# Two-layer graph network on one core: the scratch buffers of e, of adj's tiles and of the turned tiles start at multiples of 256 bytes

## The chip, the cores and the metric

The kernel runs on one core of a Trainium2 chip. The metric is the device time of one execution in microseconds (us). The core has a matrix engine (TensorE, in the profile PE, its weight loads PEld), VectorE (DVE), ScalarE (ACT), GpSimd (POOL) and the SyncE queue (SP), from which nearly all transfers are issued; 16 DMA engines carry them. On-chip memory (SBUF) has 128 partitions; a buffer takes the same byte range in each.

## The reference

The input is x (3327 nodes, 256 features) and a sparse weighted adjacency matrix adj (3327 x 3327). Layer 0 repeats two steps, each with two products: one with a fixed row-normalised matrix R made of adj, and one with an attention matrix A that is computed from the features and cut to each row's largest entries which together make 90% of its sum. Layer 1 is a masked attention of four heads over adj's neighbours.

```python
R = S + jnp.eye(N); R = R / R.sum(-1, keepdims=True)     # S is adj
for n in range(STEPS):                                   # 2 steps
    A = _top_p_attention(Xa, W1, W2, W3)                 # softmax, top-p 0.9 of each row, renormalised
    Xf = R @ Xf
    Xa = A @ Xa
    Z = Z + Xf @ U1[n].T + Xa @ U2[n].T
# layer 1
e = leaky_relu(s[:, :, None] + d[:, None, :], 0.2)       # 4 heads
attn = softmax(where(adj > 0, e, -inf), axis=2)
out = elu(einsum('hij,jhf->ihf', attn, hp))
```

## The kernel before

Rows are worked on in 26 tiles of 128 (3328 with padding). One function, `fast`, holds the whole network. It does not issue instructions as it goes: it hands pieces of work, each with an engine, an estimated length, a rank and its needs, to a planner (`Plan`), and the planner writes out one fixed order for every engine and for the SP queue. Each engine then works through its own list in that order, waiting at semaphores; nothing is reordered at run time. An engine or queue that waits holds up everything behind it in its list.

**A row tile in layer 0** goes like this. TensorE makes the logits (`logits`, L905), ScalarE their exponentials, 128 x 3328 fp32, into a buffer e (`exps`, L920). ScalarE and GpSimd look for the cut-off (`count`, L959; `before`, `step`), VectorE takes the window, sorts and drops what lies below it (`window`, `choose`, `drop`, L1075). The product with the features needs e transposed. For 49 of the 52 row tiles (`BLOCKED`) this is done in two halves: VectorE transposes 32 x 32 blocks in place (`turn_blocks`, L1112), and the blocks are then moved through HBM. For each of three column ranges (g) `put_blocks` (L1116) writes 512 KB from e to the scratch tensor `blocks`, in runs of 1024 bytes per partition and group, and `get_blocks` (L1121) brings it back in four transfers of 128 KB, each into 32 partitions, in runs of 256 bytes:

```python
src = blocks[g, :, :, o * P // 2 : (o + 1) * P // 2].rearrange("g (b s) w -> s (g b) w", b=4)
nc.sync.dma_start(self.e[part, g * PART : (g + 1) * PART].rearrange("p (c w) -> p c w", w=P // 2), src)
```

A row so takes 3 `put_blocks` and 12 `get_blocks`, and TensorE then multiplies straight from e (`attend_blocks`, L1128). There are four buffers e in the pool `epool`; every fifth row uses a fifth buffer of the same size, `qq`, in `wpool`. Besides, `Full` multiplies adj with the features (L1153): `load` (L1147) brings adj's tiles into the pool `apool` (four buffers `at` of 2048 bytes per partition). `etpool` has three buffers `et` of 2048 bytes for tiles that TensorE turned. After a row of step 0 `stage` (L1347) writes its products into one of two buffers `ystage`, whose earlier contents must have been stored by `store` (L1358) first.

**Layer 1** (`attend_neighbours`) reuses the buffers: e, `c` and `rhs` hold exponents, `qq` and `c` broadcast rows, `at` adj's tiles, `et` masks, `junk` and `y` (pool `scr`) small things.

**Where buffers lie.** Pools are laid one behind the other in the order in which they are opened, and each buffer is rounded up to a multiple of 32 bytes. In `wpool` buffers lie in the order in which their names first occur. Byte addresses within a partition in the built program, with the remainder to 256:

| buffer | before | mod 256 | after | mod 256 |
|---|---|---|---|---|
| e, four of 13312 bytes, first at | 151520 | 224 | 151552 | 0 |
| qq, 13312 bytes | 115616 | 160 | 105728 | 0 |
| at, four of 2048 bytes, first at | 214848 | 64 | 204800 | 0 |
| et, three of 2048 bytes, first at | 223040 | 64 | 212992 | 0 |
| junk (3328 bytes) | 204768 | 224 | 219136 | 0 |
| y (6752 bytes) | 208096 | 224 | 222464 | 0 |
| rhs, c, kt | 45824, 72448, 99072 | 0 | unchanged | 0 |
| ystage, two of 2048 bytes, first at | 145504 | 96 | 145536 | 128 |
| kq, three of 512 bytes, first at | 130464 | 160 | 130496 | 192 |
| qg, two of 2048 bytes, first at | 132288 | 192 | 132320 | 224 |
| base (1024 bytes) | 149856 | 96 | 149888 | 128 |

13312 and 2048 are multiples of 256, so that all buffers of a pool share the remainder.

Of the kernel before, what the change touches and what calls it, by code (L numbers as in the profile page):

```python
# [10 lines left out]
F32 = mybir.dt.float32  # L11
# [8 lines left out]
P = 128  # L20
N = 3327
NT = 26
NP = NT * P
# [564 lines left out]
def fast(  # L588
# [58 lines left out]
    with ExitStack() as l0:  # L647
        wpool = l0.enter_context(tc.tile_pool(name="wpool", bufs=1))
        small = l0.enter_context(tc.tile_pool(name="small", bufs=2))
        epool = l0.enter_context(tc.tile_pool(name="epool", bufs=4))  # L650
        scr = l0.enter_context(tc.tile_pool(name="scr", bufs=1))
        apool = l0.enter_context(tc.tile_pool(name="apool", bufs=4))
        etpool = l0.enter_context(tc.tile_pool(name="etpool", bufs=3))
        ps_l = l0.enter_context(tc.tile_pool(name="ps_l", bufs=2, space=PSUM))
        ps_a = l0.enter_context(tc.tile_pool(name="ps_a", bufs=1, space=PSUM))
        ps_x = l0.enter_context(tc.tile_pool(name="ps_x", bufs=2, space=PSUM))
# [5 lines left out]


        kt = wpool.tile([P, 3 * 512 + P], F32, name="kt")
        kks = [wpool.tile([P, P + 2], F32, name=f"kk{k}") for k in range(2)]
        for kk in kks:
            GP.memset(kk[:, :: P + 1], 1.0)
# [6 lines left out]
        for gk in gks:  # L674
            GP.memset(gk, 0.0)
            GP.tensor_copy(gk[:DA, DA + 1 :], ident[:DA, :DA])

        stat = wpool.tile([P, 2, NT], F32, name="stat")
        sig, zadd, cn, cs = (wpool.tile([P, NT], F32, name=n) for n in ("sig", "zadd", "cn", "cs"))
        met = wpool.tile([P, 6, NT], F32, name="met")  # L680
# [1393 lines left out]
def tile_gnn(tc: tile.TileContext, *args):  # L2074
    with tc.tile_pool(name="verdict", bufs=1) as pool:
        again = pool.tile([1, 1], I32, name="again")
        fast(tc, again, *args)
        with tc.If(tc.nc.values_load(again, min_val=0, max_val=1) > 0):
            general(tc, *args)
# [38 lines left out]
```

## Time and profile before

| | us |
|---|---|
| median of 3 runs (lowest to highest) | 2103.17 (2099.91 to 2103.81) |
| the profiled execution | 2100.08 |
| its span, first to last instruction | 2098.2 |
| TensorE busy | 2037.8 |
| VectorE busy | 1729.7 |
| ScalarE busy | 1300.0 |
| GpSimd busy | 990.7 |
| packets of the transfer queue, as a share of 16 engines' span | 66.4% |

The profiled execution is 3.1 us below the median, inside the spread of the runs. Busy time counts overlapping instructions once. A line of the groups reads: source line, engine, operation, what it writes and reads, shape, count, then busy time and mean duration, then the idle time of the engine just before these instructions, and what ended it.

### The profile page before, as it was taken

The numbers are of one execution on the slowest core, as the hardware profiler recorded it, in microseconds if no ns is written. First come the engines' busy times: TensorE is split into PE (matmuls) and PEld (weight loads), VectorE is DVE, ScalarE is ACT, GpSimd is POOL, SyncE is SP. The second block draws the span as 40 slices with busy tenths as digits, with TensorE's granted clock in tenths as the row PEclk, the third lists the DMA queues.
The fourth block names the chain that finished last, engine by engine and source line by source line (L and its number), as shares of the span: only waits on it lengthen the run. The fifth ranks groups of instructions, "written<-read, shape, count | busy, mean of one in ns | idle before, by whom it ended". The sixth has DMA issues, their size and how long they took to land. (4 is left out here: it accounts for less than half of the span.)

```text
span 2098.2 us, 34334 instructions
## 1 busy us (share of the span) xinstructions
PE 2037.8 (97%) x10695; PEld 1415.2 (67%) x10695; DVE 1729.7 (82%) x4105; ACT 1300.0 (62%) x2480; POOL 990.7 (47%) x2170
## 2 busy tenths in 40 slices
PE   8999999999999989989999999999999999999997
PEld 6477777878787778767878787787877333333332
DVE  5689897778876871578998979988987999999895
ACT  5767665666556621777778776778652547465552
POOL 4476654446544630567778777777772000000001
PEclk9999999999999999999999999999999999999999
DMA  4188888678877685697787888887743544453341
GB/s 116 45 190 186 194 180 195 168 152 196 189 183 172 176 186 138 199 232 165 181 189 176 203 188 191 185 191 192 182 126 89 157 141 142 125 147 115 112 127 34
DMA packets 580513, 338.56 MB, mean 161 GB/s; under 512 B 327931, under 2 KB 533281, under 8 KB 580321
## 3 DMA queue, kind: packets, MB, share of 16 engines
q1 hardware_dynamic: 579424, 336.06, 66.4%
q8 instruction: 87, 1.43, 0.3%
q14 instruction: 106, 0.86, 0.1%
q10 hardware_dynamic: 896, 0.21, 0.0%
HBM read 242.86 MB, written 93.05 MB: 160 GB/s over the span
## 5 line engine op out<-in xcount | busy, mean ns | idle before, releaser
L959 ACT ACTIVATE junk<-e,sc 128x3327 fp8e5<-128x3327 f32 x147 | 451.0, 3068 | 31.4 <-POOL sc L996 29.8
L1128 PE MATMUL acca<-rhs,e 128*128 128x256 f32 x1872 | 426.8, 381 | 4.6 <-DMA e<-blocks 4.6
L1128 PEld LDWEIGHTS acca<-rhs,e 128*128 128x128 f32 x1872 | 364.9, 197 | 48.7 <-issue 6.0
L1153 PE MATMUL accf<-c,at 128*128 128x256 f32 x1352 | 316.5, 385 | 17.1 <-DMA at<-in_adjt_dram 8.5
L1153 PE MATMUL accf<-main,at 128*128 128x257 f32 x1352 | 313.3, 381 | 5.4 <-ACT main L1304 2.5
L1153 PEld LDWEIGHTS accf<-c,at 128*128 128x128 f32 x1352 | 252.8, 192 | 67.5 <-DMA at<-in_adjt_dram 10.2
L1153 PEld LDWEIGHTS accf<-main,at 128*128 128x128 f32 x1352 | 250.4, 190 | 54.3 <-issue 11.5
L1022 DVE MAX8 cands<-y 128x8 f32<-128x205 f32 (+1 forms) x832 | 242.9, 361 | 3.6
L1918 POOL TENSOR_TENSOR qq<-qq 128x256 f32<-128x256 f32 x4 | 3.0, 759 | 457.0 <-ACT qq L1914 457.0
L1017 DVE SCALAR_TENSOR_TENSOR y<-e,sc 128x1639 f32<-128x1639 f32 x84 | 165.1, 1965 | 62.9 <-POOL sc L1007 61.7
L920 ACT ACTIVATE e<-pl 128x1024 f32<-128x1024 f32 (+1 forms) x168 | 152.9, 920 | 75.4 <-PE pl L905 74.7
L1752 ACT ACTIVATE et<-at 128x448 bf16<-128x448 f32 (+1 forms) x204 | 112.6, 552 | 128.6 <-DVE e L1763 73.3
L1779 PE MATMUL pl<-e,main 128*64 128x416 f32 x1024 | 190.4, 517 | 0.1
L1075 DVE SCALAR_TENSOR_TENSOR e<-e,thr 128x1024 f32<-128x1024 f32 (+1 forms) x168 | 178.4, 1066 | 2.4 <-DMA at<-in_adjt_dram 0.3
L905 PE MATMUL pl<-kt,qg 64*128 64x512 f32 (+1 forms) x832 | 173.7, 536 | 0.4 <-ACT qq L920 0.4
L1112 DVE STREAM_TRANSPOSE e<-e 128x1024 f32<-128x1024 f32 x117 | 146.1, 1248 | 3.7
L1779 PEld LDWEIGHTS pl<-e,main 128*64 128x64 f32 x1024 | 70.3, 137 | 111.0 <-issue 91.5
L1763 DVE SCALAR_TENSOR_TENSOR e<-c,low,et 128x832 f32<-128x832 f32 x128 | 128.8, 1070 | 6.1 <-issue 3.2
L905 PEld LDWEIGHTS pl<-kt,qg 64*128 64x128 f32 x832 | 71.5, 186 | 83.4 <-issue 76.2
L1751 ACT ACTIVATE at<-at 128x448 f32<-128x448 f32 (+1 forms) x204 | 110.8, 543 | 25.7 <-DMA at<-in_adjt_dram 25.6
L1763 DVE SCALAR_TENSOR_TENSOR e<-qq,low,et 128x832 f32<-128x832 f32 x120 | 120.5, 1073 | 4.1 <-PE accf L1793 2.9
L959 ACT ACTIVATE junk<-qq,sc 128x3327 fp8e5<-128x3327 f32 x35 | 107.4, 3068 | 10.7 <-POOL sc L996 10.4
(550 smaller groups left out, 3540.7 us busy)
## 6 DMA issues: line engine op xcount, KB each, us to landing
at<-in_adjt_dram SPq DMA_DIRECT2D x414, 256.0 KB
blocks<-e SPq DMA_DIRECT2D x117, 512.0 KB
e<-blocks SPq DMA_DIRECT2D x468, 128.0 KB
at<-in_adjt_dram SPq DMA_DIRECT2D x102, 192.0 KB
blocks<-qq SPq DMA_DIRECT2D x30, 512.0 KB
qq<-blocks SPq DMA_DIRECT2D x120, 128.0 KB
at<-in_adjt_dram SPq DMA_DIRECT2D x52, 128.0 KB
ys<-ystage SPq DMA_DIRECT2D x26, 256.0 KB
```

Of the source, the lines that this page charges most:

```text
L905: T.matmul(pl[:, lo : lo + m], qg[self.n, self.i // 4][half, self.i % 4, :], kt[half, 512 * k : 512 * k + m], start=True, stop=True,)
L920: S.activation(to, pl, AF.Exp, accum_out=(self.p0, self.p1, self.p2, self.p3)[k],)
L959: S.activation(junk[:, :N], self.e[:, :N], fn, bias=t, scale=-1.0, accum_out=dst, saturate=False)
L1017: V.scalar_tensor_tensor(self.y[:, : hi - lo], self.e[:, lo:hi], self.up, self.e[:, lo:hi], ALU.is_lt, ALU.mult, accum_out=(self.h0, self. ...
L1022: V.max(self.cands[:, a * PIECES // 2 + k, :], self.y[:, at[k] - lo : at[k + 1] - lo])
L1075: V.scalar_tensor_tensor(piece, piece, self.thr[:, o : o + 1], piece, ALU.is_gt, ALU.mult)
L1112: V.transpose(part, part)
L1128: T.matmul(self.acc, lhs, rhs[self.n][:, j, :], start=(j == 0), stop=stop and j == js[-1])
L1153: T.matmul(self.acc[:, : self.w], self.at[j // JC][:, j % JC, :], self.src[:, j, : self.w], start=(j == 0), stop=(j == NT - 1),)
L1752: S.activation(to, src, AF.Sign)
L1763: V.scalar_tensor_tensor(held["e"][:, k, :], extra["both"][b % 2][:, k, :], low[:, j, k : k + 1], held["mask"], ALU.max, ALU.mult,)
L1779: T.matmul(q["acc"][a][k * FH : (k + 1) * FH, c, :C], main[:, j, h * FH : (h + 1) * FH], held["e"][:, h, c * C : (c + 1) * C], start=(j == 0),
```

## The change

No instruction is changed, and the order of every engine and of the SP queue is the same, instruction by instruction. Only addresses differ. The pool `scr` is opened after `apool` and `etpool` instead of before them; `qq` is named right after `kt`, so that it lies behind it; and a buffer `room` of 32 bytes, which nothing uses, is put into the pool `small`, ahead of its others. The table above shows where the buffers lie before and after. Buffers of `small` move by 32 bytes.

```diff
-        scr = l0.enter_context(tc.tile_pool(name="scr", bufs=1))
         apool = l0.enter_context(tc.tile_pool(name="apool", bufs=4))
         etpool = l0.enter_context(tc.tile_pool(name="etpool", bufs=3))
+        scr = l0.enter_context(tc.tile_pool(name="scr", bufs=1))
...
         kt = wpool.tile([P, 3 * 512 + P], F32, name="kt")
+        wpool.tile([P, NP], F32, name="qq")
...
             GP.memset(gk, 0.0)
             GP.tensor_copy(gk[:DA, DA + 1 :], ident[:DA, :DA])
 
+        small.tile([P, 8], F32, name="room", bufs=1)
         stat = wpool.tile([P, 2, NT], F32, name="stat")
```

## The prediction

> **What bounds the kernel now.** I read the page's totals first, then the stretches, then TensorE's waits.
>
> ```profile
> span 2098.2 us, 34334 instructions
> PE 2037.8 (97%) x10695; PEld 1415.2 (67%) x10695; DVE 1729.7 (82%) x4105; ACT 1300.0 (62%) x2480; POOL 990.7 (47%) x2170
> ...
> L1128 PE MATMUL acca<-rhs,e 128*128 128x256 f32 x1872 | 426.8, 381 | 4.6 <-DMA e<-blocks 4.6
> ...
> L1153 PE MATMUL accf<-c,at 128*128 128x256 f32 x1352 | 316.5, 385 | 17.1 <-DMA at<-in_adjt_dram 8.5
> ```
>
> TensorE is busy for 97%. In the trace's records two of its 128x256 matmuls start 216 ns apart at the median (their 381 ns overlap), wherever their operands lie: e at 224 and qq at 160 beyond a multiple of 256, `at` at 64. So TensorE's own work is fixed, and only its idle time can shrink. The busy times of the stretches say where that is:
>
> ```profile
> 95.00:740.00 645.00, 637.06 (x2946) 501.86 (x2946) 537.25 (x1443) 416.20 (x751) 368.43 (x792) 1.00 0.80 182
> 740.00:760.00 20.00, 12.82 (x54) 11.00 (x53) 13.47 (x37) 5.09 (x5) 10.26 (x23) 0.83 0.69 166
> ...
> 895.00:1560.00 665.00, 644.01 (x3008) 522.72 (x3006) 584.10 (x1604) 496.10 (x846) 506.86 (x1100) 0.99 0.80 184
> ...
> 1575.00:2085.00 510.00, 509.41 (x3621) 207.89 (x3618) 461.83 (x583) 261.83 (x622) 14.96 (x23) 1.00 0.41 120
> ```
>
> The first numbers are the stretch's length and TensorE's busy time, the last two DMA share and GB/s. Layer 1 (1575 to 2085 us) leaves TensorE 0.6 us idle: no transfer can gain anything there. Layer 0 leaves 8 + 7 + 21 us idle in the three others shown, with DMA at 0.69 to 0.80. Who ends that idle time (us in total, times, longest):
>
> ```profile
> PE accf L1153 <- DMA at<-in_adjt_dram: 10.5, 6, 6.2
> PE px L1087 <- ACT ystage L1347: 8.5, 3, 7.2
> ...
> PE acca L1128 <- DMA e<-blocks: 4.6, 6, 1.7
> ...
> PE px L822 <- ACT ystage L1347: 0.7, 1, 0.7
> ...
> PE px L822 <- DMA qg<-kqs: 0.5, 1, 0.5
> ```
>
> 10.5 + 4.6 + 0.5 = 15.6 us end directly with a landing. The 8.5 + 0.7 = 9.2 us behind L1347 are landings too, one step removed. This is the longest:
>
> ```profile
> 743.05 0.38 SPq L1358 DMA_DIRECT2D ys<-ystage  x1
> ...
> 750.99 0.59 ACT L1347 COPY ystage<-px 128x512 f32<-128x512 f32 x1 [9.55 <-DMA ys<-ystage]
> ...
> 751.63 0.69 PE L1087 MATMUL px<-ident,e 128*128 128x128 f32 x2 [7.18 <-ACT ystage L1347]
> ```
>
> The store of `ystage` is issued at 743.05, behind the 12 `get_blocks` transfers (from 733.2) and four adj tiles, and lands nearly 8 us later; ScalarE needs the buffer, and every engine stands still meanwhile. So 15.6 + 9.2 = 24.8 us of TensorE's idle time hang on transfers. That is the most that faster transfers can bring.
>
> **What the Trainium skill says.** "DMA: Bandwidth & Descriptors", section "How a descriptor splits into AXI transactions": an aligned run goes in pieces of 256 bytes, and one that starts off a 256-byte boundary needs a piece more, whose unused part still costs 32-byte beats. The trace agrees weakly on reads: `put_blocks`, 1024 bytes a packet, has a usual median of 48 ns from e (224), 47 ns from qq (160), and packets of x into the aligned `rhs` 46 ns. Section "Where 436 GB/s comes from": a port takes 32 bytes a cycle at 850 MHz, so 256 bytes are 8 cycles, 9.4 ns. "SBUF — State Buffer", section "Door 1: The DMA port swizzle (why `[64,N]` ≈ `[32,N]`)": 32 neighbouring partitions reach 8 of 16 ports. A `get_blocks` transfer writes just 32. The same page, section "SBUF: two separate sides": engines and transfers don't contend. In line with it 216 ns stays 216 ns however DMA is loaded.
>
> **The change part by part.**
>
> *`get_blocks`, the main part.* 588 transfers, 588 x 512 = 301,056 packets of 256 bytes, more than half of all. From 224 each writes 32 bytes up to a boundary and 224 beyond, from 160 it is 96 and 160: two pieces. The packet records show a train of 12 begin with packets of 18 ns, then within about 1 us slow to a median near 31 ns with a steady 680 packets per us while nothing else runs. Over 8 ports that is 85 per us and port, 11.8 ns or 10.0 cycles: 8 for the data and, as I read it, one for each of two pieces. That reading is my inference; no aligned train is in the trace. Aligned there is one piece: 9 cycles if it still costs its one, 8 if nothing: 755 to 850 packets per us. Of a train's 6144 packets some 5000 run at the slow rate: 7.4 us now, 6.6 or 5.9 then: 0.8 to 1.5 us off each of 49 trains. A train can't go below its issue: the shortest 12 issues take 6.2 us, the mean 9.0. Bounds: 0, if the slow rate is HBM's; 1.5 us, above which the data themselves stand. I take 1.1 us.
>
> *`put_blocks`.* 147 x 512 packets, 48 to 46 ns at best: 147 x 512 x 2 / 16 = 9.4 us of 16 engines' time, 64 ns a transfer. I count 0.2 us a row and put it into the same 1.1.
>
> *`at`.* 2048 bytes from 64 take 84 ns, 86 to 88 in a backlog; aligned probably 84 to 85. 0 to 0.05 us a transfer; hidden but in the backlogs already counted. Layer 1's 512-byte packets (27 ns) lie under a TensorE with 0.6 us idle: nothing. If that cover were gone, ScalarE's wait for `at` at L1751, 25.6 us in all, would be next.
>
> *`et`, junk, y, and the engines' accesses.* `et` takes two small loads; otherwise engines use these. DVE's L1763 writes e (224) in 1070 ns and the aligned `rhs` in 1069; ACT's count reads e and qq in 3068 each. I cost these at nothing, with bounds of plus and minus 2 ns a matmul (below). The buffers of `small` stay unaligned: nothing. No wait, issue or order changes, so nothing new is queued behind anything.
>
> *What reaches TensorE.* Each stall can lose at most what its own backlog loses, or itself:
>
> - 295.5 us (1.13, adj tile behind 11 `get_blocks`): 0.9. 546.7 us (0.8, likewise): 0.8.
> - 751.6 us (7.18, above): 1.4, the train and four adj tiles.
> - 907.2 us (6.18, adj tile issued at 902.6, behind eight `get_blocks`): 0.9.
> - 1164.5 and 1243.5 us (1.72 and 1.75): 0.7 and 0.6, four to six transfers being ahead.
> - Five of 0.3 to 1.0 us behind `get_blocks` from 1301 to 1504 us and one at 739 us, 3.8 in all: 1.5, as several wait for the first landings of a train.
> - Two of 0.4 and 0.9 us behind L1347, one of 0.7 at L822, one of 0.5 behind `qg`: 0.9.
>
> Sum 7.7 us. Some of it is not kept: when TensorE is earlier, it may wait at the next point for ScalarE (`main` L1164, 5.4 us) or VectorE (3.1 us). I take off a fifth: 6 us. Against the profiled execution's own 2100.1 us (span 2098.2) that is 2094; this execution lies 3.1 us under the median of the runs, and 2103.2 - 6 = 2097 is the forecast.
>
> **The rivals.**
>
> *The straddling costs nothing that counts (same).* The slow packets could be HBM's doing: every 256 bytes are read there as well, and the same bytes were written a few us before. For it: packets that straddle into `wqk` at the start take 18 ns (but they go to 128 partitions, with no queue at a port). Against it: 10.0 cycles per port is a round number, and a train starts fast and slows, as when room in front of a full port is used up. Or the trains do get shorter, but SP's issue (9.0 us on average for 12) then sets their end. Gain 0 to 3 us: 2101 to 2103.
>
> *More than the trains' ends (faster, larger).* SP's issues slow down inside trains (504 ns median for a `get_blocks`, up to 2262): with less backlog SP runs ahead, and adj tiles behind trains start earlier as well as landing earlier. Then 12 to 16 us of the 24.8 go: 2088 to 2091.
>
> *Slower: the common phase.* Until now e, qq, `at` and `et` started at different places within 256 bytes; afterwards all start at 0, as `rhs` and `c` do. If TensorE's two reads, a weight from e or `at` and a moving row from `rhs` or `c`, met in the same part of SBUF, each of 5408 such matmuls (1872 + 480 + 352 + 1352 + 1352) would take longer. It decides from 0.8 ns each (4.3 us); 2 ns would give 10.8 us, less 6: about 2108. Against: 216 ns at the median for e at 224, qq at 160, `et` and `at` at 64, with three pairings of phases.
>
> **How the numbers follow.** Within about 0.2% (4.2 us) a measurement of this kernel can't be told from no change. The main case, 2092 to 2099, gets 0.50, the larger gain 0.12, the hidden one 0.27, the common phase 0.11. The ends of the first and third meet at 2099: a gain of 4 us. So faster 0.62, same 0.27, slower 0.11. Two in ten may be left out, so the range goes from 2089, within the larger gain, to 2105, the hidden case with the runs' own spread of 2 us; the likeliest case alone has 2092 to 2099.
>
> **What would show it.** A saturated train would run at 755 packets per us or more instead of 680, the 256-byte packets' mean fall from 27.4 ns to 20 to 24, and the queue's share from 66.4% to 60 to 64. `put_blocks` from e would show 46 ns. TensorE's wait at 751 us would end 1 to 2 us earlier after its start, those for `at` and e<-blocks sum to 7 to 11 us instead of 15.1, TensorE's busy time stay at 2038, and layer 1 keep its 510 us. The prediction fails if the rate stays at 680 (HBM then sets it), if trains shorten but TensorE's idle time reappears behind ScalarE or VectorE, or if the matmuls' spacing leaves 216 ns.

## The result and the profile after

The changed kernel takes 2083.95 us (median of 6 runs, 2080.69 to 2085.48) against 2100.62 us for the kernel before, run again beside it (6 runs, 2098.58 to 2103.81): a ratio of 0.9916, 95% interval [0.9904, 0.9929]. That is 16.7 us less, where 6 us less was forecast. The forecast time was 2097, with a range of 2089 to 2105: the direction was right, the size was not, and the time lies below the range. The 6 us had been taken off 2103.2, the median of three runs; taken off 2100.6 they lead to 2094.6, so that 2.5 us of the distance to 2097 come from the base.

The page of the kernel after, its totals and the two groups of matmuls shown before (source lines are two higher now):

```profile
span 2083.6 us, 34334 instructions
PE 2036.4 (98%) x10695; PEld 1417.9 (68%) x10695; DVE 1730.6 (83%) x4105; ACT 1298.7 (62%) x2480; POOL 999.0 (48%) x2170
...
q1 hardware_dynamic: 579424, 336.06, 57.3%
...
L1130 PE MATMUL acca<-rhs,e 128*128 128x256 f32 x1872 | 426.9, 381 | 0.6 <-DMA e<-blocks 0.3
...
L1155 PE MATMUL accf<-c,at 128*128 128x256 f32 x1352 | 315.0, 384 | 13.7 <-ACT main L1166 5.4
```

TensorE's work is what it was: 2036 us busy instead of 2038, 381 ns a matmul. The span is 14.6 us shorter, and 13.2 of these left TensorE's idle time (span less busy time: 60.4 us before, 47.2 after). The transfers carry the same bytes in 57.3% of the engines' time instead of 66.4%. TensorE's waits after the change (us in total, times, longest):

```profile
PE accf L1155 <- ACT main L1166: 5.4, 5, 3.4
PE px L1089 <- ACT ystage L1349: 5.0, 1, 5.0
PE accf L1155 <- DMA at<-in_adjt_dram: 5.0, 1, 5.0
...
PE px L824 <- DMA qg<-kqs: 2.7, 2, 1.7
...
PE acca L1130 <- DMA e<-blocks: 0.3, 1, 0.3
```

The wait behind adj's tiles fell from 10.5 us in six pieces to 5.0 in one, the one for e's blocks from 4.6 us to 0.3, the one behind `ystage` from 9.2 to 5.0. The longest stall, in order of time on SP and around it:

```profile
725.39 6.68 SPq L1123 DMA_DIRECT2D e<-blocks  x12
732.17 1.86 SPq L1149 DMA_DIRECT2D at<-in_adjt_dram  x4
734.12 0.38 SPq L1360 DMA_DIRECT2D ys<-ystage  x1
...
740.64 0.59 ACT L1349 COPY ystage<-px 128x512 f32<-128x512 f32 x1 [7.68 <-DMA ys<-ystage]
741.28 0.69 PE L1089 MATMUL px<-ident,e 128*128 128x128 f32 x2 [4.97 <-ACT ystage L1349]
```

From the first `get_blocks` to the store of `ystage` SP needs 8.7 us (734.12 - 725.39) where it needed 9.9 (743.05 - 733.19), and from that store's issue to ScalarE's start it takes 6.5 us instead of 7.9. The train helps twice: SP gets past it sooner, and what is queued behind it lands sooner.

The packet records of both traces, one row for each size that matters. A train is the 6144 packets of one row's `get_blocks`, from its first packet's start to its last one's end; its rate is the median number of packets started, over quarter-microseconds in which no packet of more than 256 bytes starts.

| | before | after |
|---|---|---|
| 256-byte packets, mean ns (median) | 27.4 (26) | 18.4 (18) |
| 1024-byte packets, mean ns (median) | 51.8 (47) | 49.1 (46) |
| 2048-byte packets, mean ns (median) | 112.4 (84) | 110.8 (84) |
| length of a train, mean of 49, us | 11.42 | 9.66 |
| SP's 12 issues, mean from the first's start to the last's end, us | 9.70 | 8.89 |
| rate of trains into e, packets per us | 680 | 912 |

In both traces the first 300 packets of a train take 18.0 ns on average. Before the change they slow down from there, to 29 ns and more after the 2000th; after it they stay at 18 to 19 ns.

### The profile page after: what moved, and what is told of

Same layout as the page of the kernel before. It is cut to its first block, busy times and chain, and to the rows that moved or that the text cites. A ratio compares the mean times of both kernels' runs of the same rounds, so it can differ in the third digit from the quotient of the medians.

```text
span 2083.6 us, 34334 instructions
## 1 busy us (share of the span) xinstructions
PE 2036.4 (98%) x10695; PEld 1417.9 (68%) x10695; DVE 1730.6 (83%) x4105; ACT 1298.7 (62%) x2480; POOL 999.0 (48%) x2170
## 3 DMA queue, kind: packets, MB, share of 16 engines
q1 hardware_dynamic: 579424, 336.06, 57.3%
## 5 line engine op out<-in xcount | busy, mean ns | idle before, releaser
L1155 PE MATMUL accf<-c,at 128*128 128x256 f32 x1352 | 315.0, 384 | 13.7 <-ACT main L1166 5.4
L1753 ACT ACTIVATE at<-at 128x448 f32<-128x448 f32 (+1 forms) x204 | 110.8, 543 | 24.7 <-DMA at<-in_adjt_dram 24.5
```

The lines of the kernel that those rows point to most:

```text
L1155: T.matmul(self.acc[:, : self.w], self.at[j // JC][:, j % JC, :], self.src[:, j, : self.w], start=(j == 0), stop=(j == NT - 1),)
```

## Experiments

All ratios are to the kernel before, run on the same chip beside the experiment. Source lines in the fences are those of the experiment's own kernel.

### Which buffers: e and qq alone, adj's and turned tiles alone

The first kernel aligns e and qq and leaves `scr` ahead of the other pools; the second aligns `at` and `et` and leaves e and qq where they were.

```diff
 # first: from the kernel before
+        wpool.tile([P, NP], F32, name="qq")
         kks = [wpool.tile([P, P + 2], F32, name=f"kk{k}") for k in range(2)]
...
+        small.tile([P, 8], F32, name="room", bufs=1)
         stat = wpool.tile([P, 2, NT], F32, name="stat")
 # second: from the kernel after
-        wpool.tile([P, NP], F32, name="qq")
-        small.tile([P, 8], F32, name="room", bufs=1)
         epool = l0.enter_context(tc.tile_pool(name="epool", bufs=4))
+        pad = l0.enter_context(tc.tile_pool(name="pad", bufs=1))
+        pad.tile([P, 8], F32, name="pad")
         apool = l0.enter_context(tc.tile_pool(name="apool", bufs=4))
```

> Only e and qq start at multiples of 256; at starts at 96 and et at 96 beyond one (64 before). Theory A, that the gain is the block trains' alone (packets of 256 bytes written across a boundary): ratio 0.991 to 0.993, mean of the 256-byte packets 18 to 19 ns, 1024-byte reads from e 46 ns, as after the whole change. Theory B, that adj's tiles bring a real part of it: 0.994 to 0.997, the rest being with at.

> Only at, et, junk and y start at multiples of 256; e stays at 224 and qq at 160. Theory A: ratio 0.998 to 1.001, 256-byte packets stay at 27 ns with 680 per us in a saturated train. Theory B: 0.994 to 0.997, mean of the 2048-byte packets down from 112 ns.

The first: 2084.01 us, ratio 0.9922 [0.9905, 0.9938], 256-byte packets 18.3 ns, train 9.36 us. The second: 2097.84 us, 0.9994 [0.9985, 1.0003], 27.8 ns, rate 678 into e. The second's waits are those of before almost unchanged:

```profile
PE accf L1155 <- DMA at<-in_adjt_dram: 9.8, 6, 5.6
PE px L1089 <- ACT ystage L1349: 7.7, 2, 6.9
PE accf L1155 <- ACT main L1166: 5.4, 5, 3.3
PE acca L1130 <- DMA e<-blocks: 4.2, 5, 1.2
```

Even TensorE's wait for `at` stays at 9.8 us with `at` aligned, and goes to 4.6 us in the first kernel, where `at` isn't. The tiles were late because of the trains ahead of them, not because of where they land. Theory A holds; adj's and the turned tiles' alignment is worth nothing that can be seen. The first kernel aligns what `put_blocks` reads as well as what `get_blocks` writes; the two were not tried apart. The packets point to the writes: 256-byte ones fell by 9 ns, the median of the 1024-byte ones by 1.

### Where a packet crosses

The four buffers e, each 32 bytes longer, start at 0, 32, 64 and 96 beyond a multiple of 256 in one kernel. `apool` and `etpool` go ahead of `epool`, so that they stay aligned.

```diff
-                    self.e = epool.tile([P, NP], F32, name="e")
+                    self.e = epool.tile([P, NP + 8], F32, name="e")[:, :NP]
```

> The four buffers e start at 0, 32, 64 and 96 beyond a multiple of 256 (each 32 bytes longer), all else as after the change. Theory A1, that a packet pays for crossing a 256-byte boundary wherever it crosses: trains into the buffer at 0 have packets of 18 ns and 900 or more per us, those at 32, 64 and 96 all have means of 26 to 30 ns and about 680 per us. Theory A2, that a start at a multiple of 64 bytes is enough (224 and 160 are none): 0 and 64 at 18 ns, 32 and 96 slow. Theory A3, that a write splits at 256 and pays by how its pieces lie: 32, 64 and 96 differ from each other by more than 2 ns. Time of the whole: 0.993 to 0.996 of before, as 20 of 39 trains into e or fewer and all 10 into qq are fast.

This kernel ran once, so the trains' numbers carry the argument. Each row of the table has 9 or 10 trains, except where it says otherwise (the last two rows are from the kernel before):

| start beyond a multiple of 256 | packets cross as | mean packet, ns | rate, packets per us |
|---|---|---|---|
| e, 0 | don't | 18.4 | 916 |
| qq, 0 | don't | 18.4 | 937 |
| e, 32 | 224 + 32 | 27.7 | 682 |
| e, 64 | 192 + 64 | 27.7 | 698 |
| e, 96 | 160 + 96 | 27.5 | 682 |
| qq, 160 (before) | 96 + 160 | 26.3 | 685 |
| e, 224 (before, 39 trains) | 32 + 224 | 27.7 | 680 |

A start at a multiple of 64 is no better than one at 32, and it hardly matters where the packet is cut. What costs is that it is cut at all: A1. The time of the one run, 2094.83 us, is near the place where 20 fast trains of 49 should put it (2100.5 - 16.5 x 20 / 49 = 2093.8, from the first kernel's gain).

### The other end of the transfer

Everything is as after the change, but `blocks` in HBM starts 32 bytes further on. The HBM tensors declared ahead of it fill multiples of 256 bytes, so it is taken to have started on a boundary until then (its address itself is not shown). `get_blocks` then reads, and `put_blocks` writes, across boundaries there.

```diff
-        blocks = spill.tile([3, 4, P, 2 * P], F32, name="blocks")
+        blocks = spill.tile([13, P, 2 * P], F32, name="blocks").rearrange("a p w -> (a p w)")
+        blocks = blocks[8 : 8 + 12 * P * 2 * P].rearrange("(r g p w) -> r g p w", r=3, g=4, p=P)
```

> All as after the change, but the scratch tensor blocks in HBM starts 32 bytes beyond a boundary, so that every 256-byte read of get_blocks and every 1024-byte write of put_blocks crosses boundaries there, while SBUF stays aligned. Theory A (the writes into SBUF pay): ratio to before 0.990 to 0.994, packets of 256 bytes at 18 to 20 ns. Rival C (a crossing costs on either side, reads too): packets of 26 ns or more, ratio 0.996 to 1.001.

2083.54 us, ratio 0.9915 [0.9899, 0.9932]; 256-byte packets 19.2 ns on average with the median still 18, rate 952 into e. Theory A holds, rival C falls: a crossing on the HBM side costs 0.8 ns a packet, on the SBUF side 9. The prediction's rival, that the slow packets were HBM's doing, fell with the change itself, which moved nothing in HBM.

### SP's issue

If trains help partly by freeing SP, then more or fewer issues for the same packets should show it. One kernel cuts each `get_blocks` in two (24 issues for a row), the other merges those of the second and third column range (8 issues).

```diff
 # 24 issues
+                for k in range(2):
+                    nc.sync.dma_start(dst[:, 8 * k : 8 * k + 8, :], src[:, 8 * k : 8 * k + 8, :])
 # 8 issues
+                if g == 1:
+                    return
+                n = 1 if g == 0 else 2
+                lo = g + 1 - n
+                src = blocks[lo : g + 1, :, :, o * P // 2 : (o + 1) * P // 2].rearrange(
+                    "r g (b s) w -> s (r g b) w", b=4
+                )
+                nc.sync.dma_start(self.e[part, lo * PART : (g + 1) * PART].rearrange("p (c w) -> p c w", w=P // 2), src)
```

> As after the change, with each get_blocks transfer cut into two of half its columns: 24 issues on SP for a row instead of 12, the same packets of 256 bytes, all of them aligned. Theory S (once a packet takes 18 ns, SP's issue sets a train's length, and what TensorE waits for hangs on it): a train's issue grows from 8.3 us to 12 or more, its span from 9.7 to 13 or more, and the time goes back to 2094 to 2104. Rival L (only the packets' own speed counts, SP has slack): spans under 11 us, time 2081 to 2088.

> As after the change, with the get_blocks of the second and third column range merged: 8 issues for a row instead of 12, four of them twice as long, which need both ranges to have been written. Theory S: issue 5.5 to 7 us, span under 9 us, time 2075 to 2081. Rival L: SP has slack and TensorE waits longer for the second range, which now comes with the third: 2083 to 2092.

With 24 issues: 2136.59 us, ratio 1.0169 [1.0141, 1.0197], slower than the kernel before, although no packet crosses and their mean is 17.6 ns. A train spans 13.25 us and its issue 13.7. SP's queue in the stretch after 100 us, and TensorE's longest waits:

```profile
105.01 11.77 SPq L1125 DMA_DIRECT2D e<-blocks  x24
```

```profile
PE accf L1157 <- DMA at<-in_adjt_dram: 13.5, 7, 6.3
PE accf L1157 <- ACT main L1168: 8.7, 6, 3.3
PE px L1089 <- DMA kt<-kqs: 8.0, 1, 8.0
```

That is theory S, and more than it expected: one issue takes 0.47 us on average, 24 of them set the train's length, and everything behind them on SP is late. Against the kernels before beside them, this one loses 37 us where the change gained 17, so the 3.6 us that each train grew cost some 54 us.

Not all of this is waiting. Here are the page's totals, and one of the stretches in which the granted clock, the share of TensorE's full clock that the records show, was halved (the stretch's length, each engine's busy time, then the granted clock, 0.50, the DMA share and GB/s):

```profile
PE 2054.5 (96%) x10695; PEld 1426.9 (67%) x10695; DVE 1730.0 (81%) x4105; ACT 1297.6 (61%) x2480; POOL 981.3 (46%) x2170
```

```profile
515.10:521.90 6.80, 6.25 (x19) 4.87 (x20) 3.13 (x7) 3.39 (x13) 5.85 (x13) 0.50 0.14 39
```

Of the 52 us by which this span (2135.5) exceeds the one after the change, 34 are idle time of TensorE (81.0 against 47.2) and 18 are busy time (2054.5 against 2036.4) for the same matmuls. Up to the end of layer 1 the granted clock was 0.50 in twelve stretches, 54 us in all, against four stretches and 17 us after the change. That the longer stalls brought these stretches about is likely, but not shown.

With 8 issues: 2089.00 us, 0.9953 [0.9938, 0.9969], a gain of 10.4 us where the change gave 16.7, and S expected more than that. The issue does shrink, only to 8.2 us from 8.9, since the longer transfers take longer to issue (0.77 us on average instead of 0.58), and the train ends hardly sooner (9.52 us). Against that the second range now waits for the third:

```profile
PE accf L1161 <- DMA at<-in_adjt_dram: 7.7, 3, 5.6
PE acca L1136 <- DMA e<-blocks: 5.1, 5, 2.2
...
PE acca L1136 <- DMA qq<-blocks: 2.7, 4, 0.9
```

That is 7.8 us of waiting for blocks where there were 0.3 after the change. Rival L is right for this direction. Taken together: SP's issue has little room to grow, as it takes about as long as the train; and here arrival in small early pieces was worth more than fewer issues.

### The order of the four partition groups, and the size of the effect

On the layout of before, the four transfers of a range go to partitions 0, 64, 32, 96 on in this order. Neighbours in the queue then reach different halves of the ports that the Trainium skill gives ("SBUF — State Buffer", section "Door 1: The DMA port swizzle (why `[64,N]` ≈ `[32,N]`)").

```diff
-                        [plan.put("SP", 0.6, rank - 1.0, row.get_blocks, g, o, needs=[b], lag=5.5) for o in range(4)]
+                        [plan.put("SP", 0.6, rank - 1.0, row.get_blocks, g, o, needs=[b], lag=5.5) for o in (0, 2, 1, 3)]
```

> As before the change (e at 224, qq at 160), but a range's four transfers go to partitions 0, 64, 32, 96 on in this order[...]. Theory P (crossing packets queue at 8 ports, 10 cycles each): saturated trains rise above 750 packets per us, mean packet under 25 ns, since neighbouring transfers overlap. Rival E (a crossing packet costs its engine the same wherever it goes): 670 to 700 per us and 27 ns. A rate that stays is weaker evidence, as transfers may hardly overlap.

> The kernel of the order 0, 64, 32, 96 on the layout of before, timed, since one look gave 2090 us with trains 0.7 us shorter (10.7 instead of 11.4 us). Theory R (TensorE's stalls are short, so that even trains a little shorter empty most of them, and the gain isn't in proportion to a train's length): ratio 0.9945 to 0.9965. Rival (the gain is in proportion, 14.6 us for 1.76): a gain of 4 to 7 us, 0.9967 to 0.998, and the look was a lucky one.

The single run: 2090.09 us, packets 25.8 ns, rates of 716 into e and 776 into qq. Six more: 2091.29 us, ratio 0.9956 [0.9940, 0.9972], and in their profile 25.7 ns, 720 and 782, and a train of 10.67 us. So the order alone, which changes no packet's crossing, gives 8.4 us. The rate into e lies between theory P's 750 and rival E's 700, the one into qq above both: which transfer follows which does matter. Several engines meeting at the same part of SBUF would explain it, but that is argued: with the order of the writes the order in which HBM is read changes too, and no run separates the two. How large that share of the slowness is stays open as well.

On the size: a train 0.75 us shorter (11.42 - 10.67) gave 8.4 us, one 1.76 us shorter 16.7 us: 11 and 9.5 us of time for each us of train. Theory R's 0.9945 to 0.9965 has the measured ratio in its middle, but the interval also takes in 0.9967, where the rival's range begins, so that "more than in proportion" is not shown. The other five kernels in this document with e and qq aligned and 12 issues a row have trains of 9.2 to 9.4 us and gains of 16.5 to 20.1, 8 to 9 us for each us. What all of them show is a slope of eight to eleven, where the prediction's own was 5.5 (6 us for 1.1).

TensorE's waits with the order changed (and packets crossing):

```profile
PE accf L1153 <- DMA at<-in_adjt_dram: 6.8, 4, 5.8
PE px L1087 <- ACT ystage L1347: 6.2, 1, 6.2
```

Now the same order on the changed layout, the small buffers of transfers aligned as well (`ystage`, `qg`, `base`, `kq` in a pool `io` of their own behind `etpool`), and both together:

```diff
+        io = l0.enter_context(tc.tile_pool(name="io", bufs=2))
         scr = l0.enter_context(tc.tile_pool(name="scr", bufs=1))
...
-                y = held["y"] = small.tile([P, 2, D], F32, name="ystage", bufs=BUFS["ystage"])
+                y = held["y"] = io.tile([P, 2, D], F32, name="ystage", bufs=BUFS["ystage"])
```

> As after the change, with the small buffers of transfers (ystage, qg, base, kq) in a pool of their own at multiples of 256 as well; e, qq, at and et stay aligned. Theory A (only packets of 256 bytes that cross a boundary matter): ratio to before as after the change, 0.990 to 0.993. Rival (longer packets and stores gain too, and the longest wait left, for ystage, shrinks by 1 us or more): 0.987 to 0.9895.

> After the change, with the order 0, 64, 32, 96. Theory P (the order helps only because crossing packets queue at 8 ports; aligned ones take 18 ns at the engine anyhow): as after the change, 0.9905 to 0.993. Rival (the order helps by itself): 0.986 to 0.989, spans of trains below 9 us.

> The small buffers of transfers aligned too, and the order 0, 64, 32, 96: the candidate for the fastest. If neither adds anything, as theories A and P have it: 0.990 to 0.993. If both do: 0.985 to 0.989.

Small buffers: 2081.86 us, 0.9921 [0.9907, 0.9934]. Order: 2081.05 us, 0.9909 [0.9893, 0.9924], packets 18.0 ns. Both: 2079.63 us, 0.9904 [0.9888, 0.9919], packets 18.0 ns. All three intervals overlap widely with that of the change itself: with the packets at 18 ns neither adds anything that these runs can tell. The last has the lowest median of all kernels, 20.1 us under the kernel before beside it, and beats that one; that it beats the change isn't shown.

## Why the prediction was wrong in size

**What bounds the kernel**: right. TensorE's work stayed (2036 us busy, 381 ns a matmul), layer 1 gave nothing (the two spans keep the same distance, 14.4 us, from 1560 us to the end), and the gain came out of the idle time tied to transfers: 24.8 us before, 13.0 after (5.0 behind `at`, 0.3 behind e's blocks, 2.7 behind `qg`, 5.0 behind `ystage`).

**`get_blocks`**: this is the first of the two terms that failed. That the crossing writes slow the trains was right, shown from three sides (e and qq alone, the four starts, HBM's side); the term was too small. 0.8 to 1.5 us off a train were worked out, 1.1 taken; it was 1.76 us. The upper bound failed: it rested on 8 ports and 850 packets per us, and the aligned trains into e run at 912, and at 952 with `blocks` moved in HBM. The measurement decides: either neighbouring transfers use both halves of the ports at times or the ports carry more; no run here separates these. The reading "8 cycles and one for each piece" falls with it: 912 packets per us over 8 ports would leave each packet 8.8 ns, less than the 9.4 that the prediction gives its data alone. (Its median near 31 ns for the slow packets is that of single stretches; over all 49 trains it is 28 to 29.) What limits the aligned trains isn't shown. 18 ns is what a 256-byte packet took at the start of a train already before, and it had been the visible floor: 63% of the packets stood above it. As an estimate from this trace, 16 engines with one packet each 18 ns start 889 packets per us, and the prediction's 5000 slow packets then take 5.6 us instead of 7.4: 1.7 us less, close to what was measured. That floor would have been the better upper bound.

**`put_blocks`** and **`at`**: as forecast. 1024-byte packets have a median of 46 ns (47 before), and `at` alone is worth nothing that can be seen.

**Engines' accesses, the rival of the common phase**: nothing of it. TensorE's spacing is 216 ns at the median in both traces. VectorE's instructions that write e in layer 1 (L1763 before) took 1078 ns on average where they took 1071; those into `rhs` and `c`, which did not move, rose alike (1068 to 1073 before, 1072 to 1082 after), and TensorE doesn't wait for them there.

**What reaches TensorE**: this is the second term that failed, and about as large an error as the first. 1.76 us off a train for 1.1 is a factor of 1.6; 14.4 us of span for each 1.76 of train, 8.2 for one, instead of the prediction's 5.5 is a factor of 1.5. All 10,695 matmuls stand in both traces in the same order, so each can be compared with itself: its start before less its start after says by how much it is earlier. The step of a stall is how much this lead grows across it:

| stalls of before (us) | forecast | measured |
|---|---|---|
| 295.5 | 0.9 | 1.3 |
| 546.7 | 0.8 | 1.0 |
| 751.6 (7.18) | 1.4 | 2.2 |
| 907.2 (6.18) | 0.9 | 1.2 |
| 1164.5 and 1243.5 | 1.3 | 3.5 |
| five from 1301 to 1504, and 739 | 1.5 | 4.0 |
| 370.8, 656.2, 689.3, 1015.1 (the last: -0.5) | 0.9 | 2.0 |
| sum | 7.7 | 15.1 |
| other stalls that shrank (470.3: 1.8; 1321.8: 1.2; ten more) | 0 | 7.5 |
| new waits (919.0: -1.7; 1256.6: -1.5; 1281.8: -0.9; six more) | -1.7 | -6.8 |
| steps under 0.25 us | | -1.4 |
| all | 6 | 14.4 |

Three things went wrong in this step. First, most stalls of 0.3 to 1.8 us behind a train were given about 0.4 of their length, and went whole or nearly so. Second, the list held only waits that the profile puts down to a landing or to `ystage`; 470.3 us (`xa`, L1319), 698.7 and others are put down to ScalarE and went too. The one at 470.3 is a landing at two removes. TensorE's stall, then ScalarE's wait ahead of it, before and after:

```profile
470.30 0.44 PE L1319 MATMUL px<-ident,xa 128*128 128x128 f32 x2 [1.63 <-ACT xa L1132]
```

```profile
464.11 0.59 ACT L1347 COPY ystage<-px 128x512 f32<-128x512 f32 x1 [3.10 <-DMA ys<-ystage]
```

```profile
460.04 0.59 ACT L1349 COPY ystage<-px 128x512 f32<-128x512 f32 x1 [1.42 <-DMA ys<-ystage]
```

ScalarE waited 1.68 us less for the store of `ystage`. Before the change it then worked without a further wait until it had made the `xa` for which TensorE stood still; with the stall gone, TensorE gained 1.79. For the other stalls put down to ScalarE this is argued, not shown. Third, a stall costs more than its gap: where 1.13 us of idle time vanished, the matmul gained 1.29, for 0.81 it was 0.98 and for 1.63 it was 1.79. The 0.16 us are 381 - 216 = 165 ns: back to back, a matmul starts that much before its forerunner's end, and the idle time counts only from that end. The fifth taken off for new waits was right in kind, and too small in us (6.8), but the gains left off the list were as large (7.5), so that it should have been nothing. The row of small steps holds stretches of halved clock, which lie elsewhere after the change: from 95.1 to 98.5 us the granted clock was 0.50 after and 1.00 before, and TensorE started 10 matmuls there where it had started 15.

**The rivals**: the larger gain (2088 to 2091, chance 0.12) was nearest and also fell short. Its reason, that SP gets past the trains sooner, was seen: the issue of 12 transfers shortened by 0.8 us, about half of the train's 1.76, and in the longest stall 1.1 us came from SP and 1.4 from landing. The range failed because the ends of the two mis-sized terms were never taken together: as an estimate, 1.5 us for 1.1 and every short stall of the prediction's list gone whole make its sum about 15 us, and 2103 less 15 is 2088, just under the range.

## What to carry to other kernels

Where a transfer writes SBUF in runs of 256 bytes, lay the buffer so that no run crosses a multiple of 256; a start at another multiple of 32 or 64 was not enough, and the HBM side mattered far less. It paid here because such packets are many and queue behind one another. For runs of 2048 bytes and for buffers that only engines use it brought nothing that could be seen; for the 1024-byte reads, which were aligned together with the writes, at most a little. When a queue in front of the bounding engine gets shorter, list every stall behind it, whatever the profile calls its releaser, let the short ones vanish whole, and add the restart of each. For what the queue can reach, take a packet's time where nothing queues.

## What the runs showed of the hardware that was not expected

- A 256-byte packet into SBUF that crosses a 256-byte boundary took 26 to 28 ns on average in trains, one that doesn't 18.4 ns, whichever of five starts from 32 to 224 it had. At the start of a train, with no queue yet, both take 18 ns: the penalty shows only in a backlog.
- The same crossing at the HBM end cost 0.8 ns (19.2 against 18.4). The Trainium skill ("DMA: Bandwidth & Descriptors", section "How a descriptor splits into AXI transactions") tells of extra beats for reads off a boundary; no run here counts beats; the writes into SBUF, of which that section doesn't speak, are what paid here, 9 ns a packet in trains.
- Aligned trains into e, 32 partitions a transfer, moved 912 to 952 packets per us, 233 to 244 GB/s, above the prediction's bound of 850 packets for 8 ports.
- The order of the four partition groups alone changed the rate of crossing packets from 680 to 720 into e and from 685 to 782 into qq, and the time by 0.4%; with aligned packets it changed the time by nothing that could be told.
- Cutting each transfer in half, at the same number of packets, cost some 54 us: 588 more issues on SP, 0.47 us each, and with them 18 us more of TensorE's busy time in stretches of granted clock 0.50.
